# Naming every place of a multi-place tile, and letting the layout choose the place

## The chip, the cores and the metric

The kernel runs on one core of a Trainium2 chip, in float32. The metric is the device time in microseconds of one execution. Three runs of the kernel before are given, and one execution was also taken by the hardware profiler.

## The reference

The input `x` has 16 sequences of 512 tokens with 256 features. It passes four blocks, each of the form `x = x + block(layernorm(x))`:

```
x = x + attention(layernorm(x))    # RMS norm, 16 heads of 16, causal softmax, output projection, its own residual
x = x + routed(layernorm(x))       # base 256x256 + rank-16 shared part + 6 rank-16 experts, the best 2 by softmax
x = x + scan(layernorm(x))         # conv over 4 tokens, silu; 16 states: h = exp(A*dt)*h + dt*x*B, y = sum(h*C); gate, projection
x = x + routed(layernorm(x))
```

## The kernel before

Tokens lie on the 128 partitions for norms, and features on them for products. The work of a sequence is cut into some 370 operations, each a Python function that issues instructions to one engine (PE, DVE, ACT, POOL or SP's DMA queue). All operations of the 16 sequences are recorded by `plan.op`, with the buffers they read and write. A long tuple, `ORDER`, found beforehand, says in which order they are issued; the scheduler of the framework keeps that order (`tc.manual_schedule()`), so on every engine the instructions stand in the order of `ORDER`. Operations of two to three sequences are woven together: the scan of one sequence beside the attention of the next.

A buffer (`Buf`) becomes a tile when the first operation on it is issued (`Buf.__call__`). Most kinds of tile have several places, for instance five for `dd` (the scan's input, 8 KB a partition) and four PSUM banks for `one` (the output of nearly every product, and the decays of the scan). The pool of the framework gives the tile a place: the one that was given back first in the order of issue. The instruction that first writes the tile then waits, by semaphores, until the last users of the earlier tile in that place are done.

`Plan.order()` also walks through `ORDER` with a model of durations (`cost`, `LAG`, `segs`), before anything is issued. The model keeps, for each kind of tile, a list `free` of the times at which its places come free, and each new buffer takes the least of them. In the kernel before this serves two ends only: an estimate of the span, and the number of *rests*.

Rests are matmuls with no use for the result (L1252): `plan.resting` puts them where the model sees PE idle, in the first 330 us and at the end, so that TensorE stays busy. There are 48. Each rest takes a tile `one`, so in the kernel before another bank each time.

The places that the prediction speaks of:

- `first()` (L583 to L587): a transpose on PE into a bank of `one`, whose result DVE turns into `bq` and `bk`; then the first 18 rests; then `turned` (L766), the transposes of the normalised `xhA` that ACT made (L755).
- `filled` (L841, L849): masks and scores of attention into the four-bank tile `sc`. DVE takes maxima of it (L947), ACT exponentials (L889). `values` (L872) weighs the values, `back` (L907) transposes them.
- `for_residual()` (L637 to L641): two copies on DVE, a product (L735) into `one`, an addition on DVE (L640) that reads it; then 5 rests and the next `filled`.
- `project` (L735 on PE, L794 on DVE): products into `one`, added to `x`. `chunked` (L779) is a product of 512 columns, L1081 a transpose in the routed block.
- `scan`: for every two groups of eight features, two DMAs on SP's queue (L1191), one for each group, spread `dt` and `dt*x` over the partitions into one `dd` tile; POOL multiplies by B (L1198); for each group ACT writes the decay into a bank of `one` (L1203) and DVE runs the recurrence over it (L1206, which reads `one`, so the bank is free when it ends); POOL multiplies by C (L1209); and PE adds up two `dd` tiles in one operation of eight rows (L1216), four for each tile. After that both `dd` tiles are free. The 32 loads of a sequence stand in one queue with the stores of `x`, `dt` and `dt*x`.

Of the kernel before, what the change touches and what calls it, by code (L numbers as in the profile page):

```python
# [334 lines left out]
class Buf:  # L335
# [4 lines left out]

    def __call__(self):
        if self.tile is None:
            self.tile = self.make()
        return self.tile


class Op:
    __slots__ = ("eng", "cost", "lat", "fn", "bufs", "needs", "seq", "num", "table", "load", "port", "stage", "segs", "next", "end")


class Plan:
# [36 lines left out]
    def order(self):  # L388
        assert sorted(ORDER) == list(range(len(self.ops)))
        out = [self.ops[k] for k in ORDER]  # L390
        free = {res: [0.0] * n for res, n in self.places.items()}
        at, runs, room, last = {}, [], [], None
        mode = table = None
        link = port = 0.0
        for o in out:
            begin = max([at.get(o.eng, 0.0), port if o.port else 0.0] + [x.end + LAG[x.eng][o.eng] for x in o.needs])
            for b in o.bufs:
                if b.place is None:
                    b.place = min(free[b.res])
                    free[b.res].remove(b.place)  # L400
                    begin = max(begin, b.place)
                    if b.res == "one":
                        room.append((begin, -1))
            cost = o.cost
            for kind, c, load in o.segs:
                cost += c + (SWITCH + load) * (kind != mode)
                mode = kind
            if o.table is not None:
                cost, table = cost + TABLE * (o.table != table), o.table
            at[o.eng] = end = begin + cost  # L410
            if o.port:
                port = end
            if o.load:
                link = max(link, end + LAND) + o.load
            o.end = link + GONE if o.load else end
            if o.eng == "PE":
                runs.append((begin, end, o))
                if last is not None:
                    last.next = o
                last = o  # L420
            for b in o.bufs:
                b.users -= 1
                b.until = max(b.until, o.end + o.lat)
                if not b.users:
                    free[b.res].append(b.until)
                    if b.res == "one":
                        room.append((b.until, 1))
        self.span = max(o.end for o in out)
        count, levels = self.places["one"], [(0.0, self.places["one"])]
        for when, change in sorted(room):  # L430
            count += change
            levels.append((when, count))
        self.rests = self.resting(runs, levels)
        return out
# [33 lines left out]
def tile_block(ctx: ExitStack, tc: tile.TileContext, a: dict, out: bass.AP):  # L468
# [61 lines left out]

    def passing(tag):

        return sb.tile([P, NC, T], F32, name=tag, tag=tag, bufs=1)

    raw = {}
    staged = None
# [1 line left out]
    def first():  # L538

        nonlocal staged  # L540
        staged = passing("oT")
        with nc.allow_non_contiguous_dma(reason="small weights, once"):
            nc.scalar.dma_start(out=nw, in_=column("norm_w"))
            nc.scalar.dma_start(out=staged[0:NJ, 0, 0 : G * HD], in_=a["bq"].rearrange("(j e) -> j e", j=NJ))
            nc.scalar.dma_start(out=staged[NJ : 2 * NJ, 0, 0 : G * HD], in_=a["bk"].rearrange("(j e) -> j e", j=NJ))
            for name, tag in (("Wk", "xc"), ("Wq", "dt"), ("Wv", "sg")):
                raw[name] = passing(tag)[:, :, 0:D]
                nc.sync.dma_start(out=raw[name], in_=chunks(name))
        nc.scalar.preload_act_table_set("exp_and_others")
        make_identity(nc, ident)  # L550
        nc.vector.memset(neg_half, -0.5)

        for mask, sign in ((mask_q, 1), (mask_k, -1)):
            nc.gpsimd.memset(mask, 0.0)
            nc.gpsimd.affine_select(
                out=mask, in_=mask, pattern=[[-sign, P]], compare_op=ALU.is_ge,
                fill=NEG, base=0, channel_multiplier=sign,
            )
        for negm in kept["negm"]:
            nc.gpsimd.memset(negm, 0.0)  # L560

        for vv in kept["vv"]:
            nc.gpsimd.memset(vv, 0.0)
            nc.gpsimd.memset(vv[:, :, :, HD : HD + 1], 1.0)
        nc.vector.tensor_copy(identb, ident)

        for s in range(2):
            rows_of = ident.rearrange("p (g s d) -> p s g d", s=2, d=HD)[:, s]
            nc.vector.tensor_reduce(half[:, s : s + 1], rows_of, AX.XY, ALU.add)
            nc.vector.tensor_reduce(first_row[:, s : s + 1], rows_of[:, :, 0], AX.X, ALU.add)  # L570
        nc.vector.tensor_scalar_mul(quarter, half, 0.25)

        spread = staged[0 : 2 * NJ, 1, 0:P].rearrange("p (g s d) -> p g s d", s=2, d=HD)
        odd = staged[0 : 2 * NJ, 1, P : P + 2]
        nc.vector.tensor_reduce(
            odd, ident[0 : 2 * NJ, 0 : 2 * NJ].rearrange("p (k s) -> p s k", s=2), AX.X, ALU.add
        )
        for s in range(2):
            nc.vector.tensor_scalar_mul(
                spread[:, :, s, :], staged[0 : 2 * NJ, 0, 0 : G * HD].rearrange("p (g d) -> p g d", g=G), odd[:, s : s + 1]  # L580
            )
        one = ps.tile([P, 512], F32, tag="one", name="one", bufs=banks["one"][0])
        nc.tensor.transpose(one[:, 0 : 2 * NJ], spread.rearrange("p g s d -> p (g s d)"), ident[0 : 2 * NJ, 0 : 2 * NJ])  # L583
        nc.vector.tensor_scalar_mul(bq, one[:, 0:NJ], 0.25)

        for s in range(2):
            nc.vector.tensor_scalar_add(  # L587
                bk.rearrange("p (i s) -> p s i", s=2)[:, s],
                one[:, NJ : 2 * NJ].rearrange("p (i s) -> p s i", s=2)[:, s], first_row[:, 1 - s : 2 - s],
            )  # L590
# [42 lines left out]
    def for_residual():  # L633

        wide = staged[:, 1, T - NC * P :].rearrange("p (c o) -> p c o", c=NC)
        for c in range(NC):
            nc.vector.tensor_copy(wide[:, c, :], staged[:, 0, T - NC + c : T - NC + c + 1].to_broadcast([P, P]))  # L637
        one = ps.tile([P, 512], F32, tag="one", name="one", bufs=banks["one"][0])
        products(one[:, 0:D], [(wide[:, c, :], wo[:, c, :], 0, D) for c in range(NC)])
        nc.vector.tensor_tensor(bo, one[:, 0:D], bo, ALU.add)  # L640
        nc.vector.tensor_scalar_mul(nwr, nwr, (1.0 + 1e-6) ** -0.5)  # L641
# [1 line left out]
    def for_routing():  # L643

        for c in range(NC):
            one = ps.tile([P, 512], F32, tag="one", name="one", bufs=banks["one"][0])
            nc.tensor.transpose(one[0:R, 0:P], shared[:, c * R : (c + 1) * R], ident)
            nc.vector.tensor_copy(turned_a, one[0:R, 0:P])
            one = ps.tile([P, 512], F32, tag="one", name="one", bufs=banks["one"][0])
            nc.tensor.matmul(one[:, 0:D], lhsT=turned_a, rhs=shared[0:R, NC * R : NC * R + D], start=True, stop=True)  # L650
            nc.vector.tensor_tensor(base[:, c, :], one[:, 0:D], base[:, c, :], ALU.add)

# [37 lines left out]
    places["drows"] = places["brows"] = 2  # L690
    plan = Plan(places)

    turns = {}

    def sbuf(name):
        n, shape = sizes[name]
        return plan.buf(name, lambda: sb.tile(shape, F32, tag=name, name=name, bufs=n))

    def psum(name):
        n, shape = banks[name]  # L700
        return plan.buf(name, lambda: ps.tile(shape, F32, tag=name, name=name, bufs=n))

    def own(name):
        def make():
            turns[name] = turns.get(name, -1) + 1
            return kept[name][turns[name] % len(kept[name])]

        return plan.buf(name, make)

    op = plan.op  # L710

# [390 lines left out]
    def scan(b, x):  # L1102
# [30 lines left out]


        dt, dx = sbuf("dt"), sbuf("sg")
        drows = plan.buf("drows", lambda: dram.tile([D, 2, T], F32, tag="drows", name="drows"))

        def chunk(i, e):
            return drows()[e * P : (e + 1) * P, i, :]
# [12 lines left out]


        bc, few = sbuf("bc"), sbuf("few")
        brows = plan.buf("brows", lambda: dram.tile([NS, 2, T], F32, tag="brows", name="brows"))
        one = psum("one")

        def tiled(one=one):
# [84 lines left out]
    with tc.manual_schedule():  # L1243
        done = 0
        for o in plan.order():

            while done < o.stage:
                setups[done]()
                done += 1
            for _ in range(plan.rests.get(o.num, 0) if done else 0):  # L1250
                one = ps.tile([P, 512], F32, tag="one", name="one", bufs=banks["one"][0])
                nc.tensor.matmul(one[:, 0 : 2 * P], lhsT=ident, rhs=ident.unsqueeze(1).to_broadcast([P, 2, P]), start=True, stop=True)  # L1252
            o.fn()

# [45 lines left out]
```

## Time and profile before

| | us |
|---|---|
| median of 3 runs | 1887.55 |
| lowest, highest | 1886.15, 1891.12 |
| the profiled execution | 1890.96 |
| its span, first to last instruction | 1889.2 |
| PE busy | 1667.1 |
| DVE busy | 1514.8 |
| POOL busy | 1451.8 |
| ACT busy | 1212.2 |

The mean granted TensorE clock of the profiled execution is 0.962 of full speed. PE's busy time counts each matmul until its modelled end, and neighbours overlap, so 1667 us is an upper reading. The page gives busy times by engine and by group of instructions, and the chain of work that ended last; further views give the waits by engine and line with what ended them, and the instructions in order of time. In the timeline a row has its start in us, its length in us, engine, line, operation, and in brackets the idle time of the engine before it with what ended that.

### The profile page before, as it was taken

The numbers are of one execution on the slowest core, as the hardware profiler recorded it, in microseconds if no ns is written. First come the engines' busy times: TensorE is split into PE (matmuls) and PEld (weight loads), VectorE is DVE, ScalarE is ACT, GpSimd is POOL, SyncE is SP. The second block draws the span as 40 slices with busy tenths as digits, with TensorE's granted clock in tenths as the row PEclk, the third lists the DMA queues.
The fourth block names the chain that finished last, engine by engine and source line by source line (L and its number), as shares of the span: only waits on it lengthen the run. The fifth ranks groups of instructions, "written<-read, shape, count | busy, mean of one in ns | idle before, by whom it ended". The sixth has DMA issues, their size and how long they took to land. (4 is left out here: it accounts for less than half of the span.)

```text
span 1889.2 us, 34803 instructions
## 1 busy us (share of the span) xinstructions
PE 1667.1 (88%) x13291; PEld 972.5 (51%) x13291; DVE 1514.8 (80%) x2448; ACT 1212.2 (64%) x1620; POOL 1451.8 (77%) x846
## 2 busy tenths in 40 slices
PE   7789899999899998989999898989999999987556
PEld 4454545555455555646465554646454554644223
DVE  4445888888798987989998788989898888887653
ACT  2346576766758686675858577675858677575541
POOL 1322878879688887879998788879898778779993
PEclk9999999999999999999999999999999999999766
DMA  4003868686676857768785767768685867777881
GB/s 104 1 1 81 200 155 214 159 203 177 171 194 157 204 152 192 187 158 212 179 216 144 191 168 195 188 173 207 153 219 151 201 152 183 177 200 203 221 218 41
DMA packets 114567, 316.47 MB, mean 168 GB/s; under 512 B 17649, under 2 KB 38626, under 8 KB 114402
## 3 DMA queue, kind: packets, MB, share of 16 engines
q1 hardware_dynamic: 113554, 313.99, 66.7%
q8 instruction: 105, 1.72, 0.4%
q14 instruction: 60, 0.49, 0.1%
q10 hardware_dynamic: 848, 0.27, 0.1%
HBM read 288.00 MB, written 26.21 MB: 166 GB/s over the span
## 5 line engine op out<-in xcount | busy, mean ns | idle before, releaser
L1198 POOL TENSOR_TENSOR dd<-dd,bc 128x1024 f32<-128x1024 f32 x256 | 604.6, 2367 | 184.6 <-DMA dd<-drows 152.8
L1206 DVE TENSOR_TENSOR_SCAN dd<-one,dd 128x512 f32<-128x512 f32 x512 | 605.7, 1210 | 121.2 <-POOL dd L1198 74.6
L1209 POOL TENSOR_TENSOR dd<-dd,bc 128x1024 f32<-128x1024 f32 x256 | 604.1, 2367 | 71.3 <-DVE dd L1206 61.0
L1203 ACT ACTIVATE one<-dd,am 128x512 f32<-128x512 f32 x512 | 348.0, 689 | 207.7 <-DVE dd L1206 78.2
L947 DVE TENSOR_REDUCE negm<-sc 128x4 f32<-128x1536 f32 (+3 forms) x224 | 368.4, 1669 | 82.1 <-PE sc L849 43.9
L849 PE MATMUL sc<-kT,qT 32*128 32x512 f32 (+3 forms) x2048 | 183.4, 461 | 23.1 <-DVE negm L947 20.8
L849 PE MATMUL sc<-qm,kT 32*128 32x256 f32 (+3 forms) x2048 | 185.5, 465 | 17.3 <-ACT ptC L889 7.2
L841 PEld LDWEIGHTS <-identb 128*128 128x128 bf16 x2048 | 120.4, 98 | 152.4 <-issue 131.9
L1216 PE MATMUL one<-dd,ysel 128*32 128x512 f32 x1024 | 157.1, 633 | 44.7 <-POOL dd L1209 38.8
L755 ACT ACTIVATE xhR<-x,nm,rs 128x256 f32<-128x256 f32 x192 | 102.4, 590 | 76.8 <-POOL nm L751 76.6
L849 PEld LDWEIGHTS sc<-kT,qT 32*128 32x128 f32 x2048 | 90.3, 184 | 110.8 <-DVE negm L947 25.4
L735 PE MATMUL one<-base,xtR 128*128 128x256 f32 x496 | 134.0, 393 | 9.9 <-DVE dd L1206 7.8
L849 PEld LDWEIGHTS sc<-qm,kT 32*128 32x128 f32 x2048 | 90.6, 185 | 97.2 <-ACT ptA L889 22.7
L889 ACT ACTIVATE ptA<-sc 128x2048 f32<-128x2048 f32 x64 | 119.9, 1874 | 27.1 <-PE sc L841 20.7
L889 ACT ACTIVATE ptB<-sc 128x2048 f32<-128x2048 f32 x64 | 120.2, 1878 | 24.0 <-PE sc L841 17.0
L794 DVE TENSOR_TENSOR x<-one,x 128x512 f32<-128x512 f32 x126 | 83.9, 675 | 34.8 <-PE one L735 34.4
L735 PEld LDWEIGHTS one<-base,xtR 128*128 128x128 f32 x496 | 92.0, 193 | 33.2 <-DVE dd L1206 12.7
L742 DVE BATCH_NORM_STATS2 st<-x 128x6 f32<-128x256 f32 x256 | 103.8, 405 | 6.2 <-DMA x<-in_x_dram 4.4
L748 POOL TENSOR_SCALAR rs<-mv 128x4 f32<-128x4 f32 x64 | 12.3, 193 | 117.1 <-DVE mv L743 108.7
L841 PE MATMUL sc<-mask_q,identb 128*128 128x128 bf16 x1024 | 84.8, 220 | 13.2 <-DVE negm L947 6.8
L799 POOL TENSOR_TENSOR x<-x,bo 128x1024 f32<-128x1024 f32 x32 | 75.5, 2361 | 23.3 <-ACT xhA L755 20.8
L841 PE MATMUL sc<-mask_k,identb 128*128 128x128 bf16 x1024 | 85.6, 222 | 2.5 <-ACT ptB L889 1.8
(147 smaller groups left out, 2780.0 us busy)
## 6 DMA issues: line engine op xcount, KB each, us to landing
dd<-drows SPq DMA_DIRECT2D x512, 512.0 KB
x<-in_x_dram SPq DMA_DIRECT2D x16, 512.0 KB
drows<-dt SPq DMA_DIRECT2D x32, 256.0 KB
drows<-sg SPq DMA_DIRECT2D x32, 256.0 KB
bc<-brows SPq DMA_DIRECT2D x16, 512.0 KB
out_dram<-x SPq DMA_DIRECT2D x15, 512.0 KB
brows<-few SPq DMA_DIRECT2D x16, 64.0 KB
wo<-in_Wo_dram SPq DMA_DIRECT2D x2, 256.0 KB
```

What stands on the lines that cost most here:

```text
L735: nc.tensor.matmul(o[:, lo:hi], lhsT=lhsT, rhs=rhs, start=n == 0, stop=n == len(todo) - 1)
L742: nc.vector.bn_stats(st()[:, t, :], x()[:, t, :])
L755: op("ACT", act(256) + 0.23, lambda t=t: nc.scalar.activation(xh()[:, t, :], x()[:, t, :], AF.Identity, bias=nm()[:, t, 0:1], scale=rs()[: ...
L841: nc.tensor.matmul(sc()[:, g, at + diag : at + diag + P], lhsT=identb, rhs=mask, start=start and k == 0, stop=False, skip_group_check=True,)
L849: nc.tensor.matmul(sc()[:, g, at : at + n], lhsT=lhsT()[rows(g), :], rhs=rhs()[rows(g), :], start=start and k == 0, stop=not start, skip_g ...
L889: op("ACT", act(G * 512) + 0.03, lambda: nc.scalar.activation(pt(), sc(), AF.Exp), r=[sc], w=[pt], table="exp")
L947: nc.vector.tensor_reduce(out, of, AX.X, ALU.max, negate=True)
L1198: op("POOL", pool(1024), lambda dd=dd: nc.gpsimd.tensor_tensor(dd()[:, :, 1, :], dd()[:, :, 1, :], both(0), ALU.mult), port=True, r=[(bc, ...
L1203: op("ACT", act(512) + 0.13, lambda i=i, k=k, dd=dd, dec=dec: nc.scalar.activation(dec(), dd()[:, i, 0, :], AF.Exp, scale=am[:, k + 4 * i ...
L1206: op("DVE", 1.13, lambda i=i, dd=dd, dec=dec: nc.vector.tensor_tensor_scan(dd()[:, i, 1, :], dec(), dd()[:, i, 1, :], 0.0, ALU.mult, ALU.a ...
L1209: op("POOL", pool(1024), lambda dd=dd: nc.gpsimd.tensor_tensor(dd()[:, :, 1, :], dd()[:, :, 1, :], both(1), ALU.mult), port=True, r=[(bc, ...
L1216: nc.tensor.matmul(sums()[rows(g), :], lhsT=ysel[:, m, :], rhs=four[g]()[:, g % 2, 1, :], start=m == 0, stop=m == 3)
```

## The change

Every place of a kind of tile gets a tag of its own in the pool (`dd0` to `dd4`, `one0` to `one3` and so on), each with one buffer. The model in `Plan.order()` keeps the number of each place beside the time at which it comes free, and notes in the buffer which place it took: the one given back first by the model's clock, and of places given back at the same time the one with the lower number. `Buf.__call__` passes that number on, so the tile is made in that place. Tiles that the setups take (`bank()`) rotate through the banks of `one` that are free at that point, and a rest takes the first of those banks. The order of the operations stays.

```diff
     def __call__(self):
         if self.tile is None:
-            self.tile = self.make()
+            self.tile = self.make(self.place)
         return self.tile
...
-        free = {res: [0.0] * n for res, n in self.places.items()}
+        free = {res: [(0.0, k) for k in range(n)] for res, n in self.places.items()}
...
+            o.spare = [k for _, k in sorted(free["one"])]
             for b in o.bufs:
                 if b.place is None:
-                    b.place = min(free[b.res])
-                    free[b.res].remove(b.place)
-                    begin = max(begin, b.place)
+                    first = min(free[b.res])
+                    free[b.res].remove(first)
+                    b.place = first[1]
+                    begin = max(begin, first[0])
...
                 if not b.users:
-                    free[b.res].append(b.until)
+                    free[b.res].append((b.until, b.place))
...
-        one = ps.tile([P, 512], F32, tag="one", name="one", bufs=banks["one"][0])
+        one = bank()
         nc.tensor.transpose(one[:, 0 : 2 * NJ], spread.rearrange("p g s d -> p (g s d)"), ident[0 : 2 * NJ, 0 : 2 * NJ])
...
-    turns = {}
+    spare = []
+
+    def bank():
+        spare.append(spare.pop(0))
+        return ps.tile([P, 512], F32, tag=f"one{spare[-1]}", name="one", bufs=1)

     def sbuf(name):
-        n, shape = sizes[name]
-        return plan.buf(name, lambda: sb.tile(shape, F32, tag=name, name=name, bufs=n))
+        return plan.buf(name, lambda k: sb.tile(sizes[name][1], F32, tag=f"{name}{k}", name=name, bufs=1))

     def psum(name):
-        n, shape = banks[name]
-        return plan.buf(name, lambda: ps.tile(shape, F32, tag=name, name=name, bufs=n))
+        return plan.buf(name, lambda k: ps.tile(banks[name][1], F32, tag=f"{name}{k}", name=name, bufs=1))

     def own(name):
-        def make():
-            turns[name] = turns.get(name, -1) + 1
-            return kept[name][turns[name] % len(kept[name])]
-
-        return plan.buf(name, make)
+        return plan.buf(name, lambda k: kept[name][k])
...
         for o in plan.order():
+            spare[:] = o.spare
             while done < o.stage:
                 setups[done]()
                 done += 1
-            for _ in range(plan.rests.get(o.num, 0) if done else 0):
-                one = ps.tile([P, 512], F32, tag="one", name="one", bufs=banks["one"][0])
+            for _ in range(plan.rests.get(o.num, 0) if done and spare else 0):
+                one = ps.tile([P, 512], F32, tag=f"one{o.spare[0]}", name="one", bufs=1)
                 nc.tensor.matmul(one[:, 0 : 2 * P], lhsT=ident, rhs=ident.unsqueeze(1).to_broadcast([P, 2, P]), start=True, stop=True)
             o.fn()
```

The DRAM buffers `drows` and `brows` get tags per place in the same way.

More of the change, by code (lines that the diff above doesn't have):

```diff
@@ L342, in __call__ @@
         if self.tile is None:
-            self.tile = self.make()
+            self.tile = self.make(self.place)
         return self.tile
 class Op:
-    __slots__ = ("eng", "cost", "lat", "fn", "bufs", "needs", "seq", "num", "table", "load", "port", "stage", "segs", "next", "end")
+    __slots__ = ("eng", "cost", "lat", "fn", "bufs", "needs", "seq", "num", "table", "load", "port", "stage", "segs", "next", "end", "spare")
 class Plan:
@@ L531, in passing @@
     def passing(tag):
-        return sb.tile([P, NC, T], F32, name=tag, tag=tag, bufs=1)
+        return sb.tile([P, NC, T], F32, name=tag, tag=f"{tag}0", bufs=1)
     raw = {}
@@ L637, in for_residual @@
             nc.vector.tensor_copy(wide[:, c, :], staged[:, 0, T - NC + c : T - NC + c + 1].to_broadcast([P, P]))
-        one = ps.tile([P, 512], F32, tag="one", name="one", bufs=banks["one"][0])
+        one = bank()
         products(one[:, 0:D], [(wide[:, c, :], wo[:, c, :], 0, D) for c in range(NC)])
@@ L645, in for_routing @@
         for c in range(NC):
-            one = ps.tile([P, 512], F32, tag="one", name="one", bufs=banks["one"][0])
+            one = bank()
             nc.tensor.transpose(one[0:R, 0:P], shared[:, c * R : (c + 1) * R], ident)
             nc.vector.tensor_copy(turned_a, one[0:R, 0:P])
-            one = ps.tile([P, 512], F32, tag="one", name="one", bufs=banks["one"][0])
+            one = bank()
             nc.tensor.matmul(one[:, 0:D], lhsT=turned_a, rhs=shared[0:R, NC * R : NC * R + D], start=True, stop=True)
@@ L1135, in scan @@
         dt, dx = sbuf("dt"), sbuf("sg")
-        drows = plan.buf("drows", lambda: dram.tile([D, 2, T], F32, tag="drows", name="drows"))
+        drows = plan.buf("drows", lambda k: dram.tile([D, 2, T], F32, tag=f"drows{k}", name="drows", bufs=1))
         def chunk(i, e):
@@ L1154, in scan @@
         bc, few = sbuf("bc"), sbuf("few")
-        brows = plan.buf("brows", lambda: dram.tile([NS, 2, T], F32, tag="brows", name="brows"))
+        brows = plan.buf("brows", lambda k: dram.tile([NS, 2, T], F32, tag=f"brows{k}", name="brows", bufs=1))
         one = psum("one")
@@ L1249, in tile_block @@
                 done += 1
-            for _ in range(plan.rests.get(o.num, 0) if done else 0):
-                one = ps.tile([P, 512], F32, tag="one", name="one", bufs=banks["one"][0])
+            for _ in range(plan.rests.get(o.num, 0) if done and spare else 0):
+                one = ps.tile([P, 512], F32, tag=f"one{o.spare[0]}", name="one", bufs=1)
                 nc.tensor.matmul(one[:, 0 : 2 * P], lhsT=ident, rhs=ident.unsqueeze(1).to_broadcast([P, 2, P]), start=True, stop=True)
```

## The prediction

> **What bounds the kernel now.** I read the head of the page, the waits by engine, SP's own queue, and then the timeline at the places that the change touches. The head says that no engine is saturated:
>
> ```profile
> span 1889.2 us, 34803 instructions
> PE 1667.1 (88%) x13291; PEld 972.5 (51%) x13291; DVE 1514.8 (80%) x2448; ACT 1212.2 (64%) x1620; POOL 1451.8 (77%) x846
> ```
>
> Three engines are at 77 to 88% and tied to each other by queues in a fixed order, so the waits between them are what there is to gain or lose. The waits (engine, line, what it waited for: total us, times, longest):
>
> ```profile
> POOL dd L1198 <- DMA dd<-drows: 152.8, 67, 22.3
> ACT one L1203 <- DVE dd L1206: 78.2, 66, 3.9
> PE one L735 <- DVE dd L1206: 14.1, 13, 3.6
> PE one L779 <- DVE dd L1206: 13.5, 15, 1.8
> PE one L872 <- DVE dd L1206: 9.7, 12, 1.7
> ...
> SPq L1191 <- PE one L1216: 866.1, 114, 20.4
> ```
>
> L735, L779 and L872 read nothing that the scan L1206 writes. They wait because the bank of `one` they write still holds a decay that L1206 reads: waits for a place. With L766, L1081, L907, L980 and L1162 the PE rows of this kind add up to 62 us. The last row, from SP's queue, is the other kind of place: 114 times the load of a `dd` stands until the matmuls L1216 have let a `dd` go, and POOL then waits for that load (first row). Both kinds are what the change rearranges.
>
> The third thing it touches is the filler matmuls ("rests", L1252), 48 in 12 groups:
>
> ```profile
> 7.63 9.89 PE L1252 MATMUL one<-ident 128*128 128x256 f32 x36
> 17.36 1.04 PE L766 MATMUL one<-ident,xhA 128*128 128x128 f32 x8
> 58.52 4.36 PE L1252 MATMUL one<-ident 128*128 128x256 f32 x10
> 62.80 1.15 PE L849 MATMUL sc<-qm,kT 32*128 32x384 f32 x16
> 64.34 1.08 PE L1252 MATMUL one<-ident 128*128 128x256 f32 x4
> 92.87 1.35 PE L1252 MATMUL one<-ident 128*128 128x256 f32 x4
> 93.53 0.30 PEld L1252 LDWEIGHTS one<-ident 128*128 128x128 f32 x2 [0.46 <-PE one L1252]
> ```
>
> A rest is two rows. 18 run back to back from 7.63, and the first transposes follow them without a gap, although their input was there: in ACT's timeline the last `xhA` row ends at 12.67 + 2.08 = 14.75. So this group is on the path already. So is the group of 5 at 58.52, whose successor starts as it ends.
>
> **The change, part by part.** The order on every engine is the same and so are the operations. What differs is which place a tile gets, and so which earlier tile it waits for. I laid the two built programs side by side. Up to the names of the places, 256 of the 1284 `one` tiles and 114 of the 256 `dd` tiles follow another tile than before; every other kind of tile keeps its predecessor, so all of `x`, `qT`, `kT`, `xtA`, `st` and the rest cost nothing. Which waits move, and by how much, I took from the ends of the rows of this trace.
>
> *Rests.* Before, the pool gave each rest another bank, so a rest waited for one several rests back. Now every rest of a group takes `o.spare[0]`, and each waits for the rest just ahead. The trace has this once: at 92.87 the second of two rests waited for the first (the row with 0.46), and the pair took 1.35 us, against 1.08 at 64.34 where it did not. Row by row the first lasted 0.595, the second started 0.06 later and lasted 0.70: a cycle of 0.76 where the group at 7.63 has 0.432 between starts. At the low clock the rows of that group are 1.22 long where one starts afresh and 0.853 apart; with the 0.06, a cycle of 1.28.
> - First group: its first rest now shares the bank of the transpose L583 and waits for L587 to read it, which ends at 8.15, so it starts at 8.25. The clock rose 3.6 us after the first matmul, so three cycles at 1.28 and 15 at 0.76: 8.25 + 3.8 + 11.4 = 23.5 instead of 17.36, +6.1.
> - Group at 58.52: the first waits for the addition L640, ended at 59.19: 59.24. Five cycles are 6.4 at the low clock, 5.4 if it rises after three: L849 at 64.6 to 65.6 instead of 62.80, +2.3 in the middle.
> - One rest at 228.78, whose bank L735 now takes next: +0.3. The last 7, at 1862.5, end at 1867.7 where L766 starts at 1867.22: +0.5.
> - The other eight groups have 0.2 to 1.2 us until the release that their successor awaits: nothing.
> Sum +9.2. What hides it? Nothing that I find in the first 95 us: only the first sequences run, each step waits for the step ahead, and the first `dd` loads hang on this chain. Bounds: 6.3 (a cycle of 0.656, from start to start at 92.87) and 10.5.
>
> [...]
>
> *Places of `dd`.* L1216 reads two `dd` tiles in one operation, the first in its first four rows. Before, the load took the tile given back first by the instruction order. In the layout both are given back at one time, and the tie goes to the lower place number, which in about half the pairs is the one read last. The load then starts 0.43 us later (the other four rows). This holds for 45 loads, by 0.1 to 0.5 us each; seven more go 0.8 to 4.0 us later, five of them after 1720, where the place taken belongs to a tile freed clearly later. What stands behind a late load on SP is the next load, now and then a store of `x` or `dt`. Set against the time between each load's landing and the first L1198 or L1203 on it, 12.6 us in 31 loads is not covered: there POOL or ACT started as the load landed. Bounds: 0 (POOL makes it up; it is idle 23% of the span) and 12.6. I take half, 6.3: POOL's wait for loads is its largest, but PE or DVE set the end over most of the chain.
>
> *Banks of `one`.* 29 PE waits get 21.6 us shorter and 28 waits of L1203 on ACT 15.6. An example:
>
> ```profile
> 1511.31 1.22 DVE L1206 TENSOR_TENSOR_SCAN dd<-one,dd 128x512 f32<-128x512 f32 x1 [1.51 <-POOL dd L1198]
> 1512.58 1.42 PE L735 MATMUL one<-base,xtR 128*128 128x256 f32 x4 [1.78 <-DVE dd L1206]
> ```
>
> L735 waited for this scan to leave its bank; now it takes one that was free, 1.73 us earlier, and the L1203 queued on ACT at 1510.08 takes the scan's bank and goes 2.45 later instead. DVE has the reduction L947 to do meanwhile, so the late side costs nothing here; elsewhere it is 0.5 us or less. Followed back through order and releases from the last instruction, the chain crosses 30 of the eased waits, 24.5 us, and two that get later, 0.5. Bounds: -24.5 (all reach the end) and 0 (each turns into the next wait). I take a third, -8: after such a wait PE soon meets the next release from DVE or ACT, and ACT's 15.6 lie beside 36% of idle time.
>
> Sum: 9.2 + 6.3 - 8.0 = +7.5. The profiled execution took 1890.96 us (span 1889.2), 3.4 above the median of 1887.55; the difference goes on the median: 1895.0. About 0.3%, 5.7 us, is what a measurement of this kernel can tell from no change.
>
> **Rivals.**
> - *The freed banks reach the end whole, and the late `dd` loads find cover.* +9.2 - 22 + 3 = -10: 1877.7, faster. For it: the chain crosses those waits, and 0.5 us of late ones. Against it: PE is idle 12% in hundreds of short gaps, and one that starts early waits in the next. It decides from the point where over 60% of the 24.5 us arrives.
> - *The parts cancel, or the places hardly matter.* 80% of the `one` tiles and 55% of the `dd` tiles keep their predecessor, and what the layout calls given back first is its own estimate, which the chip's times need not follow. With the low price of a rest, 6.3, and half of the bank waits: 6.3 + 6.3 - 12 = +0.6, 1888.
> - *Nothing of the banks arrives, and the loads count whole*: 9.2 + 12.6 = +22, 1909. For it: SP stands 866 us for places of `dd`, and a place chosen late delays every load behind it in SP's queue.
>
> **How the numbers follow.** Forecast 1895.0 for the mechanism above: 0.40; the faster rival 0.22, the cancelling one 0.20, the heavy one 0.18. Within 0.3% comes to 0.20, slower to 0.58. The range takes the forecast's own terms (9.2 between 6.3 and 10.5, the loads and banks around their middles) and half of each outer rival: 1881 to 1905.
>
> **What would show it.** Right: the first L766 near 23.5, the L849 after the second group near 65, rests 0.7 to 0.8 apart, L735 at its place near 1512 without a wait for L1206; PE's waits for L1206 down by some 20 us of 62, POOL's wait for `dd` loads up from 152.8. Wrong: the first L766 still near 17.4 (then the rests cost nothing), or POOL's wait for loads not larger while PE's idle time falls by 15 us or more (then the banks win).

## The result, and the profile after

The changed kernel took 1897.25 us (median of 9 runs, 1888.54 to 1899.27) against 1888.67 for the kernel before (9 runs). The ratio of the runs is 1.0035, with a 95% interval of 1.0019 to 1.0052: slower by 6.6 us (the two medians lie 8.6 apart), where +7.5 was forecast. The profiled execution took 1898.25 us. The total is right by luck, for its terms are not: two of them were too small by 10 and 15 us, with opposite signs, and one that cost 8 us was not in the sum at all.

The head of the page after the change:

```profile
span 1896.5 us, 34736 instructions
...
PE 1682.1 (89%) x13291; PEld 965.7 (51%) x13291; DVE 1514.7 (80%) x2448; ACT 1212.7 (64%) x1620; POOL 1454.6 (77%) x846
```

PE is "busy" 15 us longer with the same 13291 rows. PE's timeline says where (start, length in us; L1253 is a rest, two rows each):

```profile
8.29 22.95 PE L1253 MATMUL one<-ident 128*128 128x256 f32 x36 [0.60 <-DVE bk L589]
31.39 1.94 PE L766 MATMUL one<-ident,xhA 128*128 128x128 f32 x8
...
54.39 2.16 PE L1253 MATMUL one<-ident 128*128 128x256 f32 x6
...
75.96 6.34 PE L1253 MATMUL one<-ident 128*128 128x256 f32 x10 [0.52 <-DVE bo L642]
82.23 2.09 PE L849 MATMUL sc<-qm,kT 32*128 32x384 f32 x16
```

The 18 first rests took 1.275 us each to the last one, the cold cycle of the prediction (1.28), and the first L766, which the prediction put at 23.5, came at 31.39 and ran at half speed itself (1.94 instead of 1.04). The group of three at 54.39 has the warm cycle that was forecast (2.16 in all), and the group of five is cold again (the clock that the profile grants is 0.50 there; the last section has the row).

The waits (engine, line, waited for: total us, times, longest):

```profile
POOL dd L1198 <- DMA dd<-drows: 151.0, 69, 22.5
...
ACT one L1203 <- DVE dd L1206: 78.9, 62, 3.9
...
PE one L779 <- DVE dd L1206: 11.0, 10, 1.8
...
PE one L735 <- DVE dd L1206: 7.3, 8, 3.3
...
PE one L872 <- DVE dd L1206: 4.1, 8, 1.7
```

The PE rows of this kind add up to 34 us instead of 62, more than the 20 of the forecast. POOL's wait for loads did not rise. And the L735 near 1512 waits no longer for L1206:

```profile
1514.52 0.73 PEld L735 LDWEIGHTS one<-base,xtR 128*128 128x128 f32 x4 [0.84 <-DVE st L742]
1514.52 1.13 PE L735 MATMUL one<-base,xtR 128*128 128x256 f32 x4
```

All engines run the same instructions in the same order, so each can be set beside itself in the trace of before. At 100 us the changed kernel is 20.8 us late, at 500 it is 14, at 1000 it is 8, at 1600 it is 1, and at the end 9 (ends of DVE's instructions). So the start loses over twice the forecast 9.2. The rest of the kernel wins 20 us up to 1600 and loses 8 of them behind it, a net of 12, where the other two terms were to bring 1.7.

### The profile page after: what moved, and what is told of

It is laid out like the page before. It is cut to its first block, busy times and chain, and to the rows that moved or that the text cites. A ratio compares the mean times of both kernels' runs of the same rounds, so it can differ in the third digit from the quotient of the medians.

```text
span 1896.5 us, 34736 instructions
## 1 busy us (share of the span) xinstructions
PE 1682.1 (89%) x13291; PEld 965.7 (51%) x13291; DVE 1514.7 (80%) x2448; ACT 1212.7 (64%) x1620; POOL 1454.6 (77%) x846
## 5 line engine op out<-in xcount | busy, mean ns | idle before, releaser
L1206 DVE TENSOR_TENSOR_SCAN dd<-one,dd 128x512 f32<-128x512 f32 x512 | 605.9, 1211 | 135.6 <-POOL dd L1198 83.1
L849 PE MATMUL sc<-kT,qT 32*128 32x512 f32 (+3 forms) x2048 | 185.2, 464 | 23.1 <-DVE negm L947 20.0
L849 PE MATMUL sc<-qm,kT 32*128 32x256 f32 (+3 forms) x2048 | 185.1, 464 | 19.0 <-ACT ptA L889 8.5
L849 PEld LDWEIGHTS sc<-kT,qT 32*128 32x128 f32 x2048 | 90.8, 185 | 110.8 <-DVE negm L947 27.4
L849 PEld LDWEIGHTS sc<-qm,kT 32*128 32x128 f32 x2048 | 90.6, 186 | 99.8 <-ACT ptA L889 23.8
L889 ACT ACTIVATE ptB<-sc 128x2048 f32<-128x2048 f32 x64 | 120.2, 1878 | 26.8 <-PE sc L841 22.8
L735 PE MATMUL one<-base,xtR 128*128 128x256 f32 x496 | 133.3, 391 | 3.4 <-DVE x L794 1.7
L735 PEld LDWEIGHTS one<-base,xtR 128*128 128x128 f32 x496 | 91.8, 193 | 25.6 <-ACT hT L1085 5.1
```

The costliest lines, as they stand in the source:

```text
L735: nc.tensor.matmul(o[:, lo:hi], lhsT=lhsT, rhs=rhs, start=n == 0, stop=n == len(todo) - 1)
L849: nc.tensor.matmul(sc()[:, g, at : at + n], lhsT=lhsT()[rows(g), :], rhs=rhs()[rows(g), :], start=start and k == 0, stop=not start, skip_g ...
L889: op("ACT", act(G * 512) + 0.03, lambda: nc.scalar.activation(pt(), sc(), AF.Exp), r=[sc], w=[pt], table="exp")
L1206: op("DVE", 1.13, lambda i=i, dd=dd, dec=dec: nc.vector.tensor_tensor_scan(dd()[:, i, 1, :], dec(), dd()[:, i, 1, :], 0.0, ALU.mult, ALU.a ...
```

## The experiments

Each kernel was timed beside the kernel before on the same chip. Since the median of the latter lay between 1880.7 and 1888.7 us from one set of runs to the next, kernels of different sets are compared by their ratios; 0.1% is 1.9 us. "Lag" is the time of an instruction less that of the same one in the profiled execution before; it compares single executions, for some kernels on another chip, and is exact to a few us at best. Of each edit the lines that matter are shown. Line numbers in these kernels differ by a few from those of the kernel before.

**Rests and places apart.** First, only the rests are changed back:

```diff
-                one = ps.tile([P, 512], F32, tag=f"one{o.spare[0]}", name="one", bufs=1)
+                one = bank()
```

> The changed kernel, but the rests of a group go round the free banks of one, as they did before the change. Theory (read from the two traces): the rests, each waiting for the one ahead, hold the start back by some 21 us, and the places of one give back some 20 us later, independently of it. Then 1897 - 21 = 1876 us, with the first L766 near 17.4 and the body still gaining. First rival (the sizes of the prediction: rests +9.2): 1888. Second rival: the fall of the lag between 200 and 1550 us is no gain of the places but a late start caught up by a body that has slack; then the start is 14 us earlier and the end hardly moves: 1893 to 1897.

Ratio 0.9941 (0.9921 to 0.9960), median 1875.7. The first group in PE's timeline:

```profile
8.23 10.16 PE L1253 MATMUL one<-ident 128*128 128x256 f32 x36 [0.60 <-DVE bk L589]
18.23 1.04 PE L766 MATMUL one<-ident,xhA 128*128 128x128 f32 x8
```

From 85 us on its lag runs 17 to 26 us below that of the changed kernel: -1.3 at 100 us against +20.8, -13.7 at 1000 against +7.8, -15.1 at the end against +8.8. So the rests' loss reaches the end nearly whole, and the gain of the body has nothing to do with catching up. Between the ratios lie 0.94%, 18 us.

Then only `dd` is handed out by the pool again, with the rests as changed:

```diff
+        if name == "dd":
+            return plan.buf(name, lambda k: sb.tile(sizes[name][1], F32, tag=name, name=name, bufs=5))
```

> The changed kernel, but the five places of dd are handed out by the pool again (the one given back first in the order of issue). Theory: the late loads cost most after 1680 us, where the lag between the traces grows by 8 to 10 us, and a little before: 1897 - 9 = 1888 us, with the same slow rests at the start. The prediction's size for this part, 6.3: 1891. Rival: the tail loses for another reason (the banks of one, the last rests), and dd does not matter: 1896 to 1898.

Ratio 1.0023 (1.0004 to 1.0042): a gain of 0.12%, inside the intervals. The first theory had it larger. With both edits:

> Both at once: the rests go round the free banks and dd is handed out by the pool; what is left of the change is the places of one (and the names). Theory: both costs go, the gain of the banks stays: 1868 us. By the prediction's terms, banks -8: 1881. Rival (the late start is only caught up, the banks give nothing): 1888, as before the change.

0.9916 (0.9897 to 0.9934), median 1872.35: faster than the kernels before and after, and close to the 1868 of the theory. And the other half of the change, with `one` handed out by the pool (rests and setups among it, whose lines are not shown) and `dd` by the layout:

```diff
+        if name == "one":
+            return plan.buf(name, lambda k: ps.tile(banks[name][1], F32, tag=name, name=name, bufs=4))
```

> The changed kernel, but the four banks of one, those of the rests and of the setups among them, are handed out by the pool again; what is left of the change is the places of dd (and the names). Theory: only the late dd loads remain: 1889 + 9 = 1898 us, the loss mostly after 1680. The prediction's size: 1895. Rival (dd's places do not matter): 1888.

1.0053 (1.0033 to 1.0072). This looked like the price of late `dd` loads, 10 us. But beside the rests in turn, `dd` by the layout had cost only 0.25%. One of the two readings had to be wrong.

**What the order of `dd` costs.** If late loads cost 10 us, twice as many should cost about 20:

```diff
-                    free[b.res].append((b.until, b.place))
+                    turn += 1
+                    free[b.res].append((b.until, -turn if b.res == "dd" else b.place, b.place))
```

> As the kernel in which only dd follows the layout (1897.6), but of two places of dd given back at one time the one that was read last is taken first, always: 125 of the 256 tiles then follow a later tile than before the change, where with the lower number first it was 57. Theory: the price of dd is that of the late loads, in proportion: +10.3 becomes about +21, 1908 us. Rival: it comes from few places, above all the last sequence, which the two have in common: 1896 to 1900. Third: the place of dd hardly counts and the 10.3 was chance: 1888 to 1892.

1.0047 (1.0027 to 1.0067): no more than before. Either few places common to both carry the price, or the order has none. Two kernels decide. In the first, ties go to the place given back first (`turn` without the minus sign), so that every tile of every kind follows the tile that it followed before the change, and only names and addresses differ:

> Every place of every kind has its own name as in the changed kernel, except one, whose banks the pool hands out; ties between places of dd go to the one given back first. Every tile of every kind then follows the tile that it followed before the change, and every instruction waits for the same ones; only names and addresses differ. Theory: nothing, a ratio of 1.000. Rival: the 9 to 10 us of the two kernels in which dd alone follows the layout (1.0053 with 57 later predecessors, 1.0047 with 125) are not the price of dd's order at all, but of what those kernels share beside it, the names and addresses: 1.004 to 1.005.

1.0045 (1.0031 to 1.0059): the rival. In the second, ties go by number again in the last three sequences only:

> As the kernel before in one and the same order of dd, up to the 207th dd given back; after that ties go to the lower place number, as in the change: 28 tiles of the last three sequences follow another tile, 14 of them a later one. Theory: the price of dd sits where nothing comes after that could hide it, in the last sequences (five of the seven loads that go 0.8 to 4.0 us later stand after 1720): +5 us or more, 1.003 to 1.005. Rival: it is spread over the whole: under +2 us, 1.000 to 1.001.

1.0032 (1.0017 to 1.0048): inside what the theory forecast, but not above the names alone, which this kernel has too. So the order of `dd` costs between nothing and some 5 us by these pairs (0.08%, 0.25%, 0.12%, none of them separable from zero), and the names cost 8.

**Why names cost time.** A tag of its own for each place moves tiles in the on-chip memory: before, the five `dd` began at multiples of 512 bytes in each partition; with names, 128 bytes past one, as did the first `hT`, `bc` and `gate`. Some 25 other kinds of tile moved too. The page's line on the load queue (packets, MB, the time of the packets as a share of 16 engines' span), before and with names alone:

```profile
q1 hardware_dynamic: 113554, 313.99, 66.7%
```

```profile
span 1886.5 us, 34803 instructions
...
q1 hardware_dynamic: 113554, 313.99, 67.6%
```

That this span is the shorter one says nothing, since the two executions belong to different sets: in the set of this one the kernel before has a median of 1880.74 us. The price of the names is the ratio, 1.0045. The same packets and bytes took 0.667 x 1889.2 = 1260 us for each of the 16 engines before, and 0.676 x 1886.5 = 1275 with names. By the completions in the traces, a `dd` load queued behind another lands 2.15 to 2.17 us after it before the change (median, by which loads are counted as queued), and 2.18 to 2.23 in every kernel with named places. The queue's packets of 4 KB, nearly all of them `dd`, took 274 ns each before (median) and 281 to 284 in every kernel with named places. A kernel with ten rests at the start (below) has the same burden:

```profile
span 1859.6 us, 34763 instructions
...
q1 hardware_dynamic: 113554, 313.99, 68.8%
```

To this kernel I gave back the addresses by two unused tiles, with every wait as it was:

```diff
+            if name == "hT" and k not in pads:
+                pads[k] = sb.tile([P, 32 if pads else 96], F32, tag=f"pad{k}", name="pad", bufs=1)
```

> As the kernel with ten rests first (0.993 of the time before), with two unused tiles of 384 and 128 bytes a partition ahead of hT, so that hT, bc, gate and the five dd begin at multiples of 512 bytes in each partition, as they did before the change; in all kernels with named places dd began 128 bytes past one. Every wait is as in the kernel with ten rests first. In the traces a load of dd that is queued behind another lands 2.167 us after it before the change, and 2.20 to 2.23 us after it in every kernel with named places. Theory: the start of dd within 512 bytes makes the difference, and with it the 0.45% that the names alone cost: 2.17 us again, and 0.993 - 0.0045 = 0.9885. Rival: it is something else that the names move, the interval stays at 2.21 and the time at 0.993.

0.9889 (0.9861 to 0.9916), 2.15 to 2.17 us between landings, 274 ns for a packet, and

```profile
span 1855.2 us, 34763 instructions
...
q1 hardware_dynamic: 113554, 313.99, 67.8%
```

0.678 x 1855.2 = 1258 us. The interval, the packets and the queue's time are back at what they were before the change, with the names still there, so the starts in the on-chip memory made the loads slower. The time went the expected way by the expected amount; the two ratios' intervals touch, so the size rests on the names alone (0.45%), not on this pair. By which waits the slower loads reach the end is not shown: with the names alone, POOL's wait for them is 146.2 us (152.8 before), ACT's 71.9 (63.0). Why such a start costs time no run shows; what the traces show is some 0.04 us, 2%, for each load, and 7 to 10 ns for each packet of 4 KB. Starts other than these two were not tried, nor `dd` without `bc`, `gate` and `hT`.

**Why the first rests stayed slow.** Two kernels with the change as it is, but for its first group. Six rests in turn, then twelve in one bank:

```diff
+                one = bank() if many == 18 and rest < 6 else ps.tile([P, 512], F32, tag=f"one{o.spare[0]}", name="one", bufs=1)
```

> The changed kernel, but in the group of 18 rests the first six go round the free banks and only the other twelve share one bank; all other groups as changed. The question is why the first rests of the changed kernel ran at 1.28 us each to the end. Theory: rests that wait for each other do not bring TensorE up to speed, but hold the speed once it is there. Then it comes up with the six, some 3.6 us after the first, the twelve take about 0.78 each and the first L766 starts near 22 (31.4 as changed, 18.2 with all in turn); 1880 to 1885 us in all. Rival: a rest that waits is slow by itself, or the speed is lost again: the twelve take 1.28, the first L766 at 27 or later, 1890 or more.

0.9947 (0.9926 to 0.9968), 0.88% below the change, 17 us:

```profile
8.20 13.29 PE L1254 MATMUL one<-ident 128*128 128x256 f32 x36 [0.60 <-DVE bk L589]
21.64 1.06 PE L766 MATMUL one<-ident,xhA 128*128 128x128 f32 x8
```

The speed doubled at about 11.7, and the twelve waiting rests then ran at 0.755 us each and kept it. And nine wide rests in one bank instead of 18 narrow ones:

```diff
+            wide = 4 if many == 18 else 2
+            for _ in range(many * 2 // wide):
```

> The changed kernel, but the group of 18 rests of 256 columns becomes 9 of 512 columns, still all in one bank, so each waits for the one ahead. At the low speed a wide rest would hold TensorE for 1.71 of 2.13 us, 80%, where the narrow one holds it for 0.853 of 1.28, 67%. Theory: TensorE comes up to speed by the share of time in which it is held, and 67% was too little; if 80% is enough, it comes up after about two wide rests, the first L766 starts near 21, and the whole takes about 1886. Rival: a chain of waits never brings it up; 9 x 2.13 us, first L766 near 27.4, 1893.

0.9972 (0.9960 to 0.9985):

```profile
8.24 12.37 PE L1255 MATMUL one<-ident 128*128 128x512 f32 x18 [0.60 <-DVE bk L589]
20.75 1.07 PE L766 MATMUL one<-ident,xhA 128*128 128x128 f32 x8
```

The speed doubled at about 12.2, after two wide rests of 2.1 us, though each waited for the one ahead. So waiting alone does not keep the speed down. What fits all three kernels is the share of time in which TensorE is held: 81% (twice 0.853 of 2.10) brought it up, 67% (0.853 of 1.275 us) did not in 22.9 us. The wide rests also have longer rows and half as many gaps; no run separates these from the share.

**Where the banks' gain sits.** The rests in turn, `dd` by the pool, and from 1012 us on every `one` in the bank that it had before the change:

```diff
+        for b, k in zip(ones[AGAIN:], THEN):
+            b.place = int(k)
```

> As the kernel in which the rests take turns and dd is handed out by the pool (1872.35), but the banks of one follow the layout only up to the tile first used at 1012 us of the kernel before; every later tile takes the bank that it had before the change. In the trace the gain of the banks was some 13 to 14 us at 1000 us and 20 at the end. Theory: each eased wait counts where it stands and whole: the first 13 stay, the rest of the gain goes, 1872 + 6 = 1878 us. Rivals: what is won early is lost in later waits when those are as before (1885 to 1888); or only the second half matters (as before the change, 1887, minus nothing).

0.9932 (0.9917 to 0.9946). That the early gain is lost later (1885 us of 1887, 0.9988 or more) is excluded. The theory's 1878 us (0.9951) lies just outside the interval too: the later banks gave less than the 6 us expected, and that they gave anything is not shown, since the ratios do not separate this kernel from the one with all banks by the layout (0.9916). The lags do not settle it. At 1000 us, at 1600 and at the end they are -17.6, -25.4 and -17.7 here, and -13.2, -21.6 and -20.3 there, on a chip where the kernel before is some 4 us slower.

**Fewer rests at the start.**

```diff
+            for _ in range(10 if many == 18 else many):
```

> As the fastest kernel so far (rests take turns, dd handed out by the pool: 0.9916 of the time before), but with 10 rests instead of 18 in the first group, so that the transposes L766, whose input is there at 14.8, need not wait for rests that end at 18.9. Theory: the start is on the path whole, so 8 x 0.43 = 3.5 us less: 0.9916 - 0.0018 = 0.990. Rival: fewer rests leave TensorE slow in the steps after, and what is won goes there: 0.992 or more.

0.9930 (0.9914 to 0.9946). The first L766 starts at 15.31 instead of 18.92 there, but the time does not show it; with 0.9916 for 18 rests what it is worth stays open. The traces say where the lead went in this execution. It is 3.6 us up to 55 us, and 0.6 from 66 on, and between them the clock was low for longer. The stretch from 50 to 64 us with 18 rests, with ten, and with ten in the kernel with starts at 512 (length, busy us of PE, PEld, DVE, ACT, POOL, then the granted clock):

```profile
50.00:64.00 14.00, 10.85 (x81) 6.57 (x74) 8.62 (x25) 1.93 (x2) 5.69 (x6) 0.88 0.01 2
...
50.00:64.00 14.00, 12.25 (x56) 7.45 (x57) 5.06 (x20) 2.50 (x2) 8.27 (x7) 0.63 0.00 1
...
50.00:64.00 14.00, 11.57 (x84) 7.01 (x88) 4.89 (x19) 3.89 (x3) 8.62 (x7) 0.88 0.00 1
```

The third has ten rests as well, and keeps a lead of 3.8 us at 100 us. So ten rests need not cost speed later; one execution of each does not say how often they do.

## Why the prediction was right, and where it was not

*Rests, +9.2: the mechanism right, the size half.* The change back is worth 0.94% with `dd` by the layout and 1.07% with `dd` by the pool, 18 to 20 us. The step that failed is "The clock rose 3.6 us after the first matmul, so three cycles at 1.28 and 15 at 0.76": the 3.6 us belonged to rests without gaps. With gaps it did not come up in the whole group, which gives 8.29 + 18 x 1.275 = 31.2 beside the measured 31.39. The cycles themselves, 1.28 cold and 0.76 warm, were right, and so was "What hides it? Nothing": what the rests lose by 100 us is still lost at the end. The waiting rests held TensorE 67% of the time, and in 22.9 us that was too little; the two kernels with a denser start had the speed after 3.5 and 4.0 us.

*Banks of `one`, -8: the mechanism right, a third of the size.* Against the names alone (1.0045), `one` by the layout with rests in turn reaches 0.9916: -1.29%, 24 us. With `dd` by the layout it is 1.0053 to 0.9941, 21 us. The failed step is "I take a third": the end that I set aside, all of the 24.5 us that the chain crosses, is what the pairs come near to. What I held against it, that PE soon meets the next release, was no ground for two thirds. That it is those waits, one by one, that arrive is argued; the runs show the sum.

*Places of `dd`, +6.3: too much.* By the pairs, 1.5 to 5 us and not shown to be above zero. POOL's wait for loads did not rise, and doubling the late places changed nothing. "I take half" failed, in direction of the lower end.

*"Up to the names of the places": the step that was missing.* It set names and addresses to nothing. They cost 0.45%, 8.5 us. The `dd` loads became slower with the names and fast again with the starts; that these loads are the whole of the 8.5 us is argued.

So the sum is 8.5 + 19 + 3 - 23 = +7.5 by the middles of these pairs, beside the forecast +7.5 and the measured +6.6. That it meets the measured time proves nothing by itself, for the pairs are steps of one way from the kernel before to the changed one. The forecast came out right by luck: the losses that were missed (10 in the rests, 8.5 in the addresses) stood against a gain that was missed (15 in the banks) and 3 too many on `dd`. Of its signs, two came (L735 near 1512, and PE's waits, down by 28 us) and four did not (the first L766, the L849 after the second group, the pace of the first rests, POOL's wait for loads). Of the rivals, the faster one had its first condition met (well over 60% of the banks' 24.5 us arrived) and its second nearly; it failed on the rests and the addresses.

## What to carry to other kernels

Make filler that is to bring a unit to speed dense: a place chosen by a fixed index makes it a chain of waits, and here the chain that held TensorE 67% of the time left it at half speed for 22.9 us, where rests without gaps had it at full speed after 3.6. Giving tiles names also moves them, and here that made the queued `dd` loads some 2% slower (2.18 to 2.23 us between landings instead of 2.15 to 2.17): look at where the targets of the heaviest transfers begin before pricing the order of anything, and run the renaming alone as a control. When the chain of waits crosses eased waits one after another, their sum may arrive nearly whole, as here (21 to 24 us of 24.5); take a discount only for waits that a trace shows next in line.

## What the runs showed that was not expected

- The speed of TensorE depended on what had come before: twelve rests that held it 57% of the time (0.432 of 0.755 us) kept it up once it was there, and eighteen that held it 67% (0.853 of 1.275 us) did not bring it up from the low speed.
- The trace's records of the granted clock show the same, in steps. Each record but the last of a trace lasted a multiple of 3.41 us (1 to 133 times before, 1 to 254 after the change). The first record is the rise to full speed: it starts 29 and 31 us after the first rest in the two kernels with the whole chain of 18 narrow rests (at 37.7 us in the changed kernel), and 3.4 to 6.0 us after it in the twelve others. Ahead of its first record a trace has no clock, and the column of the view then reads 1.00. In the changed kernel the stretch with the slow rests lies ahead of it; the one with the cold group of five does not (stretch, length, busy us of PE, PEld, DVE, ACT, POOL, then the clock):

```profile
5.00:35.00 30.00, 25.14 (x46) 11.28 (x47) 5.07 (x24) 3.24 (x6) 2.30 (x5) 1.00 0.59 145
...
72.00:85.00 13.00, 10.86 (x38) 5.67 (x39) 1.98 (x9) 0.25 (x1) 8.39 (x6) 0.50 0.00 0
```

- 128 bytes in the start of the tiles made loads of 512 KB slower by some 0.04 us each. There are 512 of them; with the names alone the queue's packets took 15 us more on each engine, and the kernel 8.5.
- The version with the lowest ratio, named places with rests in turn, `dd` by order of return, ten rests first and starts at multiples of 512 bytes, takes 0.9889 of the time before; its interval overlaps that of 18 rests without the starts (0.9916).
